# One decoder layer on one core: the values of key groups 0 and 1 as one Strassen product, and another order at the seam of the last two groups

## The chip, the cores and the metric

The kernel runs on one core of a Trainium2 chip. The metric is device time in microseconds for one launch, lower being better. The time before is 1264.26 us, the median of three runs (1264.23 to 1265.07).

## What is computed

One transformer layer on a sequence of 1024 tokens of width 512, all in float32: attention with 32 query heads and 8 key/value heads of 128 (four query heads share one key head, a group), rotary embedding and a causal mask; an addition and a layer norm; a gated feed-forward block of 1792; an addition and a second layer norm. Cut to what matters here:

```python
q = (x @ wq).reshape(B, T, H, HD).transpose(0, 2, 1, 3)
k = (x @ wk).reshape(B, T, KV, HD).transpose(0, 2, 1, 3)
v = (x @ wv).reshape(B, T, KV, HD).transpose(0, 2, 1, 3)
q = q * cos + _rotate_half(q) * sin
k = k * cos + _rotate_half(k) * sin
k = jnp.repeat(k, H // KV, axis=1)
v = jnp.repeat(v, H // KV, axis=1)
scores = jnp.einsum('bhtd,bhsd->bhts', q, k) * (1.0 / np.sqrt(HD))
scores = jnp.where(mask, scores, -jnp.inf)
att = jax.nn.softmax(scores, axis=-1)
out = jnp.einsum('bhts,bhsd->bhtd', att, v)
out = out.transpose(0, 2, 1, 3).reshape(B, T, H * HD) @ wo
x = _layernorm(x + out)
x = _layernorm(x + ffn(x))
```

## The kernel before

**Projections by Strassen's form.** The sequence is cut into two halves of 512 columns (blocks of 128 tokens, the odd ones in the first half, the even ones in the second) and the width of 512 into two halves. `blocks` holds a11, a12, a22 and four sums s1 to s4 of x; s3 lies over a21. `project_two(s)` (line 487) makes a pair of heads or groups from one product of two 2x2 block matrices: seven products in the order 1, 2, 6, 5, 3, 7, 4, each of two chunks of 128, with sums u1 to u4 of the weights. `weigh(s)` (line 262) makes u1, u2 and u3 on GpSimd; u4 follows after product 2. `steps` is the list of such pairs, `load(s)` fetches the weights of one. A product is added up by VectorE (`put`, lines 513 to 558), its first one copied by ScalarE (line 544). For values the operands are swapped, so that each product is 4 blocks of 128 columns.

**Plain projections.** The pairs in `PLAIN` (heads 0 to 3 of group 0, heads 2 and 3 of group 7), the keys of groups 0 and 7, and the values of groups 0 and 1 are made without it, half by half: `project_queries`, `project_keys` (with `rotate`, three VectorE instructions and a GpSimd add), and `values(g, even)` (line 375), each half of which is 4 blocks of 4 chunks of 128 columns, one ScalarE copy (line 391) and, after the first half, a GpSimd subtract of the weights (`difference`, line 284).

**Attention.** For each of 8 groups, the eight blocks of 128 queries are taken in the order 7, 1, 5, 3, 4, 2, 6, 0 (`ORDER`; p is the place in it, i the block). A block has four tiles t = 4i to 4i+3 of 32 tokens by 4 heads. `scores` (line 589) makes one tile: score matmuls into one of two PSUM buffers (`pair`), VectorE's masked minimum (line 609), ScalarE's exponential (626), VectorE's reciprocal (630), ScalarE's scaling (631) and a VectorE transpose by 32 x 32 blocks (634) into the buffer `turned`. When a block's four tiles are there, `gather` issues 16 DMAs on SyncE (line 684) that bring it from `turned` to `moved`, where two blocks lie at a time (`place`). After landing, matmuls with v make `o`, ScalarE copies it (856), and a pair of blocks is multiplied with wo (`project_pair`) and added to `sums`.

**Order.** TensorE's matmuls keep the program's order; the other engines' instructions are ordered by the framework's scheduler at build time, within the limits of dependencies and `issue_after`. A planner written out in the kernel chooses the program's order. It counts in units: one unit is one product of 128 x 128 by 512 columns. `Early` holds the projections that are still to be made for the next group, `Late` the blocks whose gather is under way. After each tile's scores, `run` (groups 0 to 5) or `deal` (groups 6 and 7) takes units from both. `weight` spreads the work over the 32 tiles of a group: the tile t gets 1 - share + 2 share (t + 1) / 33, with share 0.25 and, in the last two groups, 0.5. `make_room(g, p, i)` finishes all blocks whose place in `moved` the block i will take; it is called ahead of the block's last tile. Group 6 keeps three pairs of blocks (`held`) for group 7, which has no projections of a next group, to fill its time with.

**Start.** Before the attention loop come the first half of heads 0 to 3 and both halves of group 0's keys, then `values(0, 0)`. The other three halves of the values, and the second half of the heads, run between the first tiles. The three sums s3, s2 and s4 (line 1016) are made by VectorE as block p = 1 of group 0 begins.

Of the kernel before, what the change touches and what calls it, by code (L numbers as in the profile page):

```python
# [31 lines left out]
ALU = mybir.AluOpType  # L32
# [3 lines left out]
P = 128  # L36
# [4 lines left out]
KV = 8  # L41
HD = 128
REP = HEADS // KV
INNER = 1792
NT = T // P
# [26 lines left out]

HEAVY = 33 + 36 + NT // 2 * PAIR


# [19 lines left out]
def kernel(  # L95
# [88 lines left out]
    with ExitStack() as att:  # L184
# [66 lines left out]

        steps = []
        for g in range(KV - 2):
# [116 lines left out]

        current = added = None

        SOME = NT // 2 * NC * HD / W

        def values(g, even):

            nonlocal added
            if g not in vs:
                vs[g] = piece(f"v{g}").rearrange("p (j f) -> p j f", j=NT)
            pv = mbank(f"v_ps{g}_{even}")  # L380
            for j in range(NT // 2):
                for c, (w, x) in enumerate(operands(wvs[g], even)):
                    matmul(
                        pv[:, j * HD : (j + 1) * HD],
                        lhsT=x[:, j * P : (j + 1) * P],
                        rhs=w,
                        start=(c == 0),
                        stop=(c == NC - 1),
                    )
                if j == NT // 2 - 1:  # L390
                    nc.scalar.copy(
                        vs[g][:, 1 - even :: 2, :], pv.rearrange("p (j f) -> p j f", f=HD)
                    )
                    if not even:

                        with tc.issue_after(added.ins):
                            added = difference(wvs[g])
                yield NC * HD / W

# [4 lines left out]
        def rotate(dst, src, even, name):  # L404

            nonlocal added
            ts = slice(even * W, (even + 1) * W)
            b = ap.tile([P, W], F32, tag="rope_b", name=f"{name}_b{even}")


            def swapped():
                for to, of in ((slice(0, 64), slice(64, P)), (slice(64, P), slice(0, 64))):
                    nc.vector.tensor_tensor(
                        alike(b, dst)[to], src[of], alike(sin[:, ts], dst)[of], ALU.mult
                    )

            nc.vector.tensor_tensor(dst, src, alike(cos[:, ts], dst), ALU.mult)
            swapped()
            added = nc.gpsimd.tensor_tensor(dst, dst, alike(b, dst), ALU.add)
# [60 lines left out]
        def project_queries(g, head, even):  # L480
            dst = queries(g, even)[:, :, head, :]
            yield from project(dst, wqs[g * REP + head], even, f"q{g}_{head}", g > 0)
            if g == 0 and even and head % 2:
                load(head // 2 + 1)

        def project_two(s):
# [34 lines left out]
            for k, w, x in products:  # L521
# [21 lines left out]
                if k == 1:  # L543
                    nc.scalar.copy(v, ps[1])
                elif k == 2:
                    nc.gpsimd.tensor_tensor(u4, b21, u2, ALU.subtract)
                    put(c := out(0, 0), ps[2], alike(v, c))
                    done(0, 0)
                elif k == 6:
                    nc.vector.tensor_tensor(v, ps[6], v, ALU.add)  # L550
                elif k == 5:
                    put(c := out(1, 0), ps[5], alike(v, c))
                elif k == 3:
                    put(c := out(1, 0), ps[3], c)
                    done(1, 0)
                    weigh(s + 1)
                elif k == 7:
                    nc.vector.tensor_tensor(v, ps[7], v, ALU.add)
                    put(c := out(1, 1), ps[5], alike(v, c))
                    done(1, 1)  # L560
                else:
                    put(c := out(0, 1), ps[4], alike(v, c))
                    done(0, 1)
                    if s:
                        load(s + 2)
                yield 1

        def projections(g):


            s, pieces = 3 * (g - 1), []
            if g < KV - 1:
                pieces.append((PAIR * 2, project_two(s)))
            else:
                pieces += [(NC, project_keys(g, even)) for even in range(2)]
            for n in (2 * g, 2 * g + 1):
                s += 1
                if n in PLAIN:
                    pieces += [(NC, project_queries(g, 2 * (n % 2) + h, 0)) for h in range(2)]
                else:  # L580
                    pieces.append((PAIR * 2, project_two(s)))
            return pieces
# [316 lines left out]
        now = queue = 0.0  # L899
        late, tiles = deque(), []  # L900

# [35 lines left out]
        def run(g, until, early, pace, must=0, least=0, limit=None):  # L937
# [22 lines left out]
            while early.done < must:  # L960
                now += early.step()

        for piece_of in (
            project_queries(0, 0, 0),
# [4 lines left out]
            project_queries(0, 3, 0),  # L969
            values(0, 0),  # L970
        ):
            for _ in piece_of:
                pass

        with tc.issue_after(added.ins):
            for a in range(REP):
                added = difference(wqs[a])
        list(first_keys)
        weigh(0)
        for g in range(KV):  # L980
            todo, own, odd = [], 0, math.inf
            if g == 0:
                todo += [(SOME, values(*which)) for which in ((0, 1), (1, 0), (1, 1))]
            for a in range(REP):
                if (g * REP + a) // 2 in PLAIN:
                    todo.append((NC, project_queries(g, a, 1)))
# [11 lines left out]
            slots = T // Q  # L998
            slot = (early.total - own + HEAVY) / slots

            share = 0.25 if g < KV - 2 else 0.5
            weight = [1 - share + share * 2 * (t + 1) / (slots + 1) for t in range(slots)]
# [3 lines left out]
            for p, i in enumerate(ORDER):  # L1006

                for n in {0: (0,) if g % 2 else (0, 2), 4: (1,)}.get(p, ()):
                    while chores[n]:
                        current = current or chores[n]  # L1010
                        chore()
                if g == KV - 1 and p == 1:
                    load_wo(g)
                if g == 0 and p == 1:
                    for a in ((s3, a11, a21), (s2, s1, a11), (s4, a12, s2)):
                        chores[0].append(lambda a=a: nc.vector.tensor_tensor(*a, ALU.subtract))
                if g == 0 and 0 < p <= NT // 2:
# [6 lines left out]
                for b in range(B):  # L1024
                    t = i * B + b
                    if b == B - 1:
                        make_room(g, p, i)
# [3 lines left out]
                    now += (t + 1) * Q / W  # L1031
                    if b == B - 1:
                        tiles.append(Late(g, i, gather(g, p, i, x), now, unturned))
                        late.append(tiles[-1])
                    due += slot * weight[t]
                    passed += weight[t]
# [7 lines left out]
                    else:  # L1044
                        limit = early.total - (KEPT if g == KV - 1 else 0)
                        coming = [
                            ((k + 1) * B + LAG - done, Late.units(g, ORDER[k]))
                            for k in range(p + (b == B - 1), len(ORDER))
                        ]
# [423 lines left out]
```

## Time and profile before

| what | us |
|---|---|
| median of three runs | 1264.26 |
| the profiled execution | 1267.03 |
| its span, first to last instruction | 1265.2 |
| TensorE busy in it | 1247.5 |
| VectorE busy | 881.4 |
| ScalarE busy | 466.2 |
| GpSimd busy | 471.9 |
| mean granted TensorE clock | 0.997 |

The projections before the loop take the first 31 us, group 0 goes on to about 130 us, the seam of groups 6 and 7 lies near 875 us, the last scores near 975 us, the feed-forward block between 1005 and 1265 us. A line of the timeline gives start, length, engine, line, operation, names and count, and in brackets how long the engine had been idle and what ended it; matmuls are issued from one helper and all carry line 135. A list of waits gives total, number of times and the longest. A busy engine need not be at its peak: matmuls are pipelined and their ends are modelled.

### The profile page before, as it was taken

Reading aid. Unit: us, or ns where it says so; the run is one execution under the profiler, and the core shown is the slowest. Engines: PE = TensorE matmul, PEld = TensorE weight load, DVE = VectorE, ACT = ScalarE, POOL = GpSimd, SP = SyncE. Lnnn points to the kernel's source line nnn. Section 1 sums busy time; section 2 is a strip of 40 time slices with the busy share of each in tenths; the row PEclk is TensorE's granted clock in tenths of the full one; section 3 lists DMA queues with packets and bytes.
Section 4 is the critical chain, followed back from the end, with each engine's and each line's share of the span. In section 5 each row is a group of like instructions: output and inputs, shape, how many; then the busy total and the mean of one; then the engine's idle time right before and its main releaser. Section 6 shows DMA issues by size and latency. Waiting matters only on the chain. (4 is left out here: it accounts for less than half of the span.)

```text
span 1265.2 us, 14259 instructions
## 1 busy us (share of the span) xinstructions
PE 1247.5 (99%) x4142; PEld 735.9 (58%) x4142; DVE 881.4 (70%) x1821; ACT 466.2 (37%) x922; POOL 471.9 (37%) x708
## 2 busy tenths in 40 slices
PE   9999999999999999999999999999999999999998
PEld 5644676565456755655567555554656744444887
DVE  4677786887778767877796778687765674436743
ACT  0443344434443444444444444454555111111000
POOL 3541333343434233425341424253320756543321
PEclk9999999999999999999999999999999999999999
DMA  8243235433534344334433433544443711110000
GB/s 274 47 121 92 52 80 140 105 83 83 134 94 99 78 116 103 90 82 124 99 84 87 132 91 68 133 118 108 99 100 92 209 34 51 50 34 1 17 17 34
DMA packets 89326, 115.55 MB, mean 91 GB/s; under 512 B 18464, under 2 KB 60192, under 8 KB 89248
## 3 DMA queue, kind: packets, MB, share of 16 engines
q1 hardware_dynamic: 88240, 112.66, 35.4%
q10 hardware_dynamic: 1008, 1.97, 0.4%
q8 instruction: 34, 0.56, 0.2%
q14 instruction: 44, 0.36, 0.1%
HBM read 37.23 MB, written 2.10 MB: 31 GB/s over the span
## 5 line engine op out<-in xcount | busy, mean ns | idle before, releaser
L626 ACT ACTIVATE p<-s,low 128x928 f32<-128x928 f32 (+31 forms) x256 | 179.2, 700 | 362.1 <-DVE low L609 351.8
L634 DVE STREAM_TRANSPOSE turned<-p 128x1024 f32<-128x1024 f32 (+7 forms) x244 | 186.8, 775 | 101.5 <-ACT p L631 62.4
L135 PE MATMUL o<-moved,v 128*128 128x512 f32 x550 | 255.1, 597 | 0.0
L631 ACT ACTIVATE p<-p,share 128x928 f32<-128x928 f32 (+31 forms) x256 | 187.3, 735 | 120.8 <-DVE share L630 120.8
L609 DVE CUSTOM_DVE_ANT_0 s<-s,mask 128x928 f32<-128x928 f32 (+31 forms) x256 | 179.0, 700 | 56.5 <-PE s L135 54.8
L135 PE MATMUL s<-k,queries 128*128 128x512 f32 (+15 forms) x576 | 204.0, 464 | 2.3 <-ACT p L626 2.3
L135 PEld LDWEIGHTS s<-k,queries 128*128 128x128 f32 x576 | 108.5, 191 | 108.5 <-issue 96.3
L135 PEld LDWEIGHTS o<-moved,v 128*128 128x128 f32 x550 | 103.0, 191 | 104.5 <-issue 98.3
L135 PE MATMUL q_p<-blocks,wq 128*128 128x512 f32 x260 | 123.7, 594 | 0.0
L440 POOL TENSOR_TENSOR queries<-queries,q_b 128x512 f32<-128x512 f32 x52 | 71.3, 1371 | 122.1 <-DVE queries L439 115.6
L624 POOL MEMSET p<- 128x96 f32 (+2 forms) x192 | 26.3, 151 | 212.1 <-DVE turned L634 186.9
L135 PE MATMUL y<-wo,oT 128*128 128x256 f32 x428 | 103.7, 381 | 0.0
L135 PEld LDWEIGHTS y<-wo,oT 128*128 128x128 f32 x428 | 79.8, 190 | 21.5 <-issue 7.8
L434 DVE TENSOR_TENSOR q_b<-queries,sin 64x512 f32<-64x512 f32 x104 | 84.4, 811 | 3.1
L630 DVE RECIPROCAL share<-total 128x1 f32<-128x1 f32 x256 | 39.6, 155 | 57.7 <-ACT p L626 55.6
L135 PEld LDWEIGHTS q_p<-blocks,wq 128*128 128x128 f32 x260 | 48.4, 190 | 46.3 <-issue 40.5
L135 PE MATMUL s<-kT,queries 128*128 128x512 f32 (+8 forms) x192 | 68.3, 466 | 4.7 <-ACT p L626 4.7
L781 DVE TENSOR_TENSOR sums<-y,sums 128x512 f32<-128x512 f32 x112 | 66.9, 607 | 4.2 <-PE y L135 3.2
L135 PE MATMUL y<-u,os 128*128 128x256 f32 x224 | 57.5, 390 | 1.6 <-POOL os L760 1.6
L135 PEld LDWEIGHTS s<-kT,queries 128*128 128x128 f32 x192 | 35.7, 190 | 39.7 <-issue 29.2
L135 PE MATMUL q_p<-blocks,uq 128*128 128x512 f32 x104 | 49.8, 592 | 0.0
L626 ACT ACTIVATION_READ_ACCUMULATOR p<-s,low 128x1 f32 x256 | 49.5, 193 | 0.0
(273 smaller groups left out, 1771.2 us busy)
## 6 DMA issues: line engine op xcount, KB each, us to landing
moved<-turned SPq DMA_DIRECT2D x112, 128.0 KB, 2.4
moved<-turned SPq DMA_DIRECT2D x128, 112.0 KB, 2.2
moved<-turned SPq DMA_DIRECT2D x112, 96.0 KB, 2.2
moved<-turned SPq DMA_DIRECT2D x112, 80.0 KB, 2.1
wo<-wo SPq DMA_DIRECT2D x16, 512.0 KB, 4.5
moved<-turned SPq DMA_DIRECT2D x128, 64.0 KB, 2.0
wq<-wq SPq DMA_DIRECT2D x14, 512.0 KB, 4.4
moved<-turned SPq DMA_DIRECT2D x128, 48.0 KB, 1.9
```

Source lines behind the costliest of these rows:

```text
L135: tc.keep_in_program_order(nc.tensor.matmul(*args, **kw))
L434: nc.vector.tensor_tensor(alike(b[0], dst)[to], dst[of], alike(sin[:, ts], dst)[of], ALU.mult)
L440: nc.gpsimd.tensor_tensor(dst, dst, alike(b[0], dst), ALU.add)
L609: extreme = nc.vector.tensor_tensor_reduce(out=s[:, :n], in0=s[:, :n], in1=mask[:, T - n :], scale=1.0, scalar=MASKED, op0=ALU.add, op1=AL ...
L624: cleared = nc.gpsimd.memset(p[:, n:full], 0.0)
L626: nc.scalar.activation(p[:, :n], s[:, :n], AF.Exp, bias=low, scale=-1.0, accum_out=total)
L630: nc.vector.reciprocal(share, total)
L631: last_of_all = nc.scalar.activation(p[:, :n], p[:, :n], AF.Copy, scale=share)
L634: nc.vector.transpose(x[:, :, :, b, :].rearrange("p b j q -> p j b q"), p[:, :full].rearrange("p (j b k) -> p j b k", b=B, k=Q),)
L781: pin(nc.vector.tensor_tensor(to, out, to, ALU.add))
```

## The change

The values of groups 0 and 1 become the first entry of `steps`, so that every later index is one higher. `values` goes; `project_two(0)` takes its place: two of its seven products (four calls of `next`) ahead of the loop, the rest (10 units) between the first tiles. `weigh(0)` now makes the sums for the values, ahead of them, and `weigh(1)` those for the next pair. The sums s3 and s2 move to VectorE's place behind the rotations of the first half of the keys and of their second half, tied there by `issue_after`; s4 is handed to the first tile's chores. In the seam, `narrow` tells in groups 6 and 7 whether a block's place still holds more than one unit of unfinished work; if so, `make_room` and `gather` wait until the next block's first tile has its scores (`waiting`, which also carries over from group 6 to group 7). Of the two plain half-heads that group 7 made in its own time, the second half of head 2 moves into group 6; that of head 3 stays. The share in the last two groups goes from 0.5 to 0.1, and from group 1 on the work that `slot` spreads is 4 units larger (`AHEAD`).

```diff
@@ -71,6 +71,8 @@
+AHEAD = 4
@@ -249,7 +251,8 @@
-        steps = []
+        steps = [("v", 0, 1)]
         for g in range(KV - 2):
@@ -368,34 +371,7 @@
-        current = added = None
-        SOME = NT // 2 * NC * HD / W
-        def values(g, even):
-            nonlocal added
-            if g not in vs:
-                vs[g] = piece(f"v{g}").rearrange("p (j f) -> p j f", j=NT)
-            pv = mbank(f"v_ps{g}_{even}")
-            for j in range(NT // 2):
-                for c, (w, x) in enumerate(operands(wvs[g], even)):
-                    matmul(
-                        pv[:, j * HD : (j + 1) * HD],
-                        lhsT=x[:, j * P : (j + 1) * P],
-                        rhs=w,
-                        start=(c == 0),
-                        stop=(c == NC - 1),
-                    )
-                if j == NT // 2 - 1:
-                    nc.scalar.copy(
-                        vs[g][:, 1 - even :: 2, :], pv.rearrange("p (j f) -> p j f", f=HD)
-                    )
-                    if not even:
-                        with tc.issue_after(added.ins):
-                            added = difference(wvs[g])
-                yield NC * HD / W
+        current = added = moved = None
@@ -403,14 +379,15 @@
-            nonlocal added
+            nonlocal added, moved
             ts = slice(even * W, (even + 1) * W)
...
             def swapped():
+                nonlocal moved
                 for to, of in ((slice(0, 64), slice(64, P)), (slice(64, P), slice(0, 64))):
-                    nc.vector.tensor_tensor(
+                    moved = nc.vector.tensor_tensor(
                         alike(b, dst)[to], src[of], alike(sin[:, ts], dst)[of], ALU.mult
@@ -481,7 +458,7 @@
             if g == 0 and even and head % 2:
-                load(head // 2 + 1)
+                load(head // 2 + 2)
@@ -553,7 +530,8 @@
                     done(1, 0)
-                    weigh(s + 1)
+                    if s:
+                        weigh(s + 1)
                 elif k == 7:
@@ -561,14 +539,14 @@
                     done(0, 1)
-                    if s:
+                    if s > 1:
                         load(s + 2)
...
-            s, pieces = 3 * (g - 1), []
+            s, pieces = 3 * (g - 1) + 1, []
             if g < KV - 1:
@@ -576,7 +554,9 @@
                 if n in PLAIN:
-                    pieces += [(NC, project_queries(g, 2 * (n % 2) + h, 0)) for h in range(2)]
+                    which = (2, 0), (3, 0), (2, 1)
+                    pieces += [(NC, project_queries(g, *which_of)) for which_of in which]
                 else:
@@ -897,7 +877,15 @@
         now = queue = 0.0
-        late, tiles = deque(), []
+        late, tiles, waiting = deque(), [], None
+        def narrow(g, p, i):
+            if g < KV - 2 or g == KV - 1 and p == NT - 1:
+                return False
+            there = place(g, p, i)
+            return sum(l.left for l in tiles if not l.weighed and overlap(l.place, there)) > 1
@@ -960,6 +948,7 @@
+        sums_of_x = [1, (s3, a11, a21), (s2, s1, a11)]
         for piece_of in (
@@ -967,22 +956,35 @@
             project_queries(0, 3, 0),
-            values(0, 0),
         ):
...
+            if sums_of_x:
+                wait = sums_of_x[0]
+                if wait:
+                    sums_of_x[0] -= 1
+                else:
+                    with tc.issue_after(moved.ins):
+                        nc.vector.tensor_tensor(*sums_of_x[1], ALU.subtract)
+                    sums_of_x = [1] + sums_of_x[2:] if sums_of_x[2:] else []
+        weigh(0)
+        first_values = project_two(0)
+        for _ in range(4):
+            next(first_values)
...
         list(first_keys)
-        weigh(0)
+        weigh(1)
         for g in range(KV):
...
             if g == 0:
-                todo += [(SOME, values(*which)) for which in ((0, 1), (1, 0), (1, 1))]
+                todo.append((PAIR * 2 - 4, first_values))
             for a in range(REP):
-                if (g * REP + a) // 2 in PLAIN:
+                if (g * REP + a) // 2 in PLAIN and (g == 0 or a == REP - 1):
                     todo.append((NC, project_queries(g, a, 1)))
@@ -996,9 +998,9 @@
             slots = T // Q
-            slot = (early.total - own + HEAVY) / slots
-            share = 0.25 if g < KV - 2 else 0.5
+            slot = (early.total - own + HEAVY + (0 if g else AHEAD)) / slots
+            share = 0.25 if g < KV - 2 else 0.1
             weight = [1 - share + share * 2 * (t + 1) / (slots + 1) for t in range(slots)]
@@ -1009,11 +1011,10 @@
                         chore()
+                if g == 0 and p == 0:
+                    chores[0].append(lambda: nc.vector.tensor_tensor(s4, a12, s2, ALU.subtract))
                 if g == KV - 1 and p == 1:
                     load_wo(g)
-                if g == 0 and p == 1:
-                    for a in ((s3, a11, a21), (s2, s1, a11), (s4, a12, s2)):
-                        chores[0].append(lambda a=a: nc.vector.tensor_tensor(*a, ALU.subtract))
                 if g == 0 and 0 < p <= NT // 2:
@@ -1023,15 +1024,22 @@
                     t = i * B + b
-                    if b == B - 1:
+                    if b == B - 1 and not narrow(g, p, i):
                         make_room(g, p, i)
...
                     now += (t + 1) * Q / W
-                    if b == B - 1:
-                        tiles.append(Late(g, i, gather(g, p, i, x), now, unturned))
+                    if waiting or b == B - 1 and not narrow(g, p, i):
+                        g_of, p_of, i_of, x_of, at = waiting or (g, p, i, x, now)
+                        make_room(g_of, p_of, i_of)
+                        y, at = gather(g_of, p_of, i_of, x_of), max(at, now - TURNED)
+                        tiles.append(Late(g_of, i_of, y, at, unturned))
                         late.append(tiles[-1])
+                        waiting = None
+                    elif b == B - 1:
+                        waiting = g, p, i, x, now
                     due += slot * weight[t]
@@ -1045,7 +1053,7 @@
                             ((k + 1) * B + LAG - done, Late.units(g, ORDER[k]))
-                            for k in range(p + (b == B - 1), len(ORDER))
+                            for k in range(p + (b == B - 1 and not waiting), len(ORDER))
                         ]
```

## The prediction

> **What bounds the kernel now.** The page's first part says where to look: TensorE is busy nearly throughout.
>
> ```profile
> PE 1247.5 (99%) x4142; PEld 735.9 (58%) x4142; DVE 881.4 (70%) x1821; ACT 466.2 (37%) x922; POOL 471.9 (37%) x708
> ```
>
> So only two things can shorten it: fewer matmuls, or less time in which TensorE stands. The list of TensorE's waits gives the second.
>
> ```profile
> PE s L135 <- ACT p L626: 7.0, 4, 2.3
> PE y L135 <- POOL os L760: 1.6, 5, 0.4
> PE v_ps L135 <- POOL wv L284: 0.4, 1, 0.4
> ```
>
> Four waits of a score matmul for the exponential two tiles back (the `pair` tag has two PSUM buffers) make 7.0 us. TensorE's timeline places them, with the work that the change removes (start, length, engine, instructions; in brackets the idle time before).
>
> ```profile
> 32.50 2.84 PE L135 MATMUL v_ps<-wv,blocks 128*128 128x128 f32 x24
> 35.18 1.77 PE L135 MATMUL s<-kT,queries 128*128 128x512 f32 x4
> ...
> 43.94 1.60 PE L135 MATMUL v_ps<-wv,blocks 128*128 128x128 f32 x12 [0.41 <-POOL wv L284]
> ...
> 58.83 1.40 PE L135 MATMUL s<-kT,queries 128*128 128x512 f32 x4 [0.65 <-ACT p L626]
> ...
> 862.48 4.46 PE L135 MATMUL o<-moved,v 128*128 128x512 f32 x10
> 866.77 1.81 PE L135 MATMUL s<-k,queries 128*128 128x512 f32 x6
> 870.90 1.06 PE L135 MATMUL s<-k,queries 128*128 128x64 f32 x4 [2.32 <-ACT p L626]
> 871.75 4.12 PE L135 MATMUL o<-moved,v 128*128 128x512 f32 x6
> ...
> 901.44 0.82 PE L135 MATMUL s<-kT,queries 128*128 128x224 f32 x2 [1.87 <-ACT p L626]
> ...
> 968.18 1.02 PE L135 MATMUL o<-queries,v 128*128 128x512 f32 x2
> ...
> 971.51 0.73 PE L135 MATMUL s<-kT,queries 128*128 128x64 f32 x4 [2.17 <-ACT p L626]
> ```
>
> An instruction here is half a float32 product (two passes), so x24 is twelve calls; the planner's unit is two passes of 512 columns. Three of the four waits lie in the seam of groups 6 and 7. Cutting the span into stretches shows a second loss there (each row: stretch, length, busy time of PE, PEld, DVE, ACT and POOL, then the granted clock).
>
> ```profile
> 865.00:875.00 10.00, 7.68 (x20) 4.02 (x19) 7.47 (x20) 4.90 (x14) 1.72 (x4) 0.83 0.22 52
> 900.00:910.00 10.00, 8.56 (x29) 6.61 (x30) 6.22 (x21) 5.04 (x14) 3.15 (x8) 0.83 0.77 170
> 965.00:975.00 10.00, 7.83 (x25) 4.01 (x24) 5.12 (x17) 6.48 (x16) 0.00 (x0) 1.00 0.10 25
> ```
>
> After the stalls of 2.32 and 1.87 us the clock falls: 0.17 x 10 us = 1.7 us lost each time (the six `o` passes at 871.75 cover 4.12 us; the same count at 972.21 covers 2.81). After 2.17 us it does not. The seam thus holds 6.36 us of idle time and 3.4 us of half clock.
>
> **The change part by part.** The sum is made on the profiled execution, 1267.03 us (span 1265.2); the median shown is 2.77 lower, and I carry the difference over.
>
> *Values.* Before: 4 halves x 4 blocks x 4 chunks = 64 products, 128 passes. After: 7 products x 4 blocks x 2 chunks = 56, 112 passes. The 24 passes from 32.50 give way to a score at 35.18: 2.68/24 = 0.112 us. 16 x 0.112 = **-1.79 us**. Nothing else on TensorE is added or removed.
>
> *Waits that go with it.* `difference(wvs[1])` vanishes, and with it the 0.41 us at 43.94. The three subtracts of line 1016 took 1.77 + 1.22 + 2.09 = 5.08 us of VectorE between 50.5 and 60.2, just ahead of the stall of 0.65 us at 58.83; two now run before the scores and the third during tile 28. Between 0 and -0.65; I take all, because VectorE was between two of them when that stall built up. Together **-1.06**.
>
> *The price at the start.* `s3` and `s2` now stand on VectorE among the first rotations, behind k0's and k1's. Its idle gaps there are 1.17 us (before 23.92) and 1.34 (before 27.35), 2.51 together; the two subtracts need 2 x 1.22 = 2.44. That hides them with nothing to spare: queued behind them are the rotations of q1, k1, q2, q3, and for q3's the first score at 30.84 waits, which today starts 0.1 us after the `v_ps` passes end. If a GpSimd add gets in first, a subtract takes up to 2.09 (the longest of the three), 0.9 more each. On GpSimd, `weigh(0)` puts three subtracts (0.80 + 0.83 + 0.80, lines 277 to 279) where q3's add (29.53 to 30.79) is due; its gap before that add is 2.17 us, partly usable, so 0 to 1.5 us. `u4` (0.8) and one difference of 0.73 fewer hide in GpSimd's idle 63%; uncovered they would delay the wq differences, which TensorE needs only at 48.8. ScalarE loses four copies of 0.59 and gains one. VectorE gains seven adds of 0.69 (line 514's rows) and `s4`, 6.0 to 6.6 us, in the four widest tiles: their reductions (4 x 1.3), reciprocals and transposes (4 x 1.25) make 10.8, together some 17.2 us in the 17.3 from 32.7 to 50. Full, but a score is two buffers deep. Bounds 0 and +3.8 (0.9 x 2 + 1.5 + 0.5 for lag); I take **+0.8**, near the covered end, since every wait named has room today. The DMAs keep their order: `steps` grows by one and every index with it; weights of v0 and v1 were loaded before too.
>
> *Seam, stall at 870.90.* Today `make_room` runs ten `o` passes (4.29 us) before score 27, nothing stands between scores 27, 0 and 1, and score 1 waits for the exponential of 27. With `narrow` true there (five units of tile 4 unweighed), score 27 goes ahead and the ten passes land between scores 0 and 1. From the end of score 27 (868.4) to its release (870.9) is 2.5 us; 4.29 covers that. Lost: 2.32 idle and 1.7 of clock. What is late next is scores 2 and 3, now with thinner cover: 0.5. **-3.5**, bounds -4.0 and 0.
>
> *Stall at 901.44.* Score 6 waits for VectorE, which runs four transposes of 1024 columns in one go:
>
> ```profile
> 895.97 4.62 DVE L634 STREAM_TRANSPOSE turned<-p 128x1024 f32<-128x1024 f32 x4 [0.24 <-issue]
> ```
>
> Their buffer is free once tile 6's gather has been read: 16 DMAs at 0.63 us, 10.1 us on SyncE from 873.35. Score 27 is some 4 us earlier after the change, hence its last transpose and that gather too. But group 7's own projections shrink from 8 to 4 units (head 2 moves to group 6: 8 passes, 3.44 us, with its rotation of 2.1 us and its add of 1.3), so scores 28 to 31 also come sooner, and the four transposes may bunch again. Bounds -3.6 (1.87 + 1.7) and 0; I take half, **-1.8**.
>
> *Stall at 971.51.* `narrow` is not true there; only `share` 0.1 helps. The weight of tile 0 rises from 0.52 to 0.91 and that of tile 27 falls from 1.35 to 1.07, so that one unit (0.86 us) should fall between scores 0 and 1. Bounds -2.17 and 0; **-0.9**.
>
> *Deferred gathers and AHEAD.* A deferred gather is issued after one more score and its fill, some 3.3 us (99 us of group 7 over 32 tiles). On SyncE the next gather, and group 7's `wo` load, queue behind it; but the gather waits for the fourth transpose anyway (873.35 against score 27's end at 868.4), which hides most of it. AHEAD lifts the middle groups' rate from 139/32 to 143/32 units a tile; their rows are busy 119.5 us in 120, so little is there to win or lose. Bounds -0.5 and +6 (two gathers uncovered); **+1.0**.
>
> Sum: -1.79 - 1.06 + 0.8 - 3.5 - 1.8 - 0.9 + 1.0 = **-7.25**: 1259.8 for an execution like the profiled one, **1257.0** for the median.
>
> [...]
>
> **Rivals.** *The seam gives nothing* (its stalls only move): -1.79 - 1.06 + 0.8, that is 1262.2. For it: work there is conserved, and fill is what was lacking. Against it: ten passes demonstrably stand on the wrong side of score 27.
>
> *The seam gives all:* -2.05 - 4.0 - 3.6 - 2.2 = 1252.4. Against it: the third stall has no new cover but the flatter weights.
>
> *Slower, by the transposes at group 7's start.* If tile 6's gather does not begin earlier, scores 28 to 31 arrive 3.44 us sooner at transposes that stay where they are, the deferral adds 3.3, and the stall at 901.44 grows by 6.7 and drags a second slow window (1.7). With the first stall's gain kept: -2.05 - 3.5 + 8.4 = +2.9, 1267.1. It decides once the last transpose of tile 27 is less than about 3 us earlier relative to score 28. For it: today's four in a row. Against it: score 27 moves by 4.29.
>
> *That the change doesn't do what it says* would show as 128 passes still; the loop counts exclude it.
>
> **How the numbers follow.** Forecast 52% (own range 1253 to 1261), seam gives nothing 22%, gives all 11%, slower 15%. A difference under 0.2% (2.5 us) can't be told from none. Faster: 0.50 + 0.09 (a seam that gives a little) + 0.11 = 0.70; same 0.15; slower 0.15. The range 1251.5 to 1265 leaves out the slower case and a few per cent below.
>
> **What would show it.** 112 passes of `v_p` before group 1's, no wait on `wv`, no idle over 0.5 us before 60; ten `o` passes between scores of 32 and 64 columns near 860; no stretch at clock 0.83; four transposes no longer in a row near 892. First scores later than 31.5, or a wait over 2 us on `L626` in groups 6 and 7, would make it wrong.

## The result, and the profile after

| | before | after |
|---|---|---|
| median, us | 1265.54 (six runs, 1264.23 to 1266.67) | 1260.12 (six runs, 1259.84 to 1260.50) |
| profiled execution, us | 1267.03 | 1259.86 |
| its span, us | 1265.2 | 1257.8 |
| mean granted TensorE clock | 0.997 | 0.999 |

The ratio of the times is 0.9956, with a 95% interval of 0.9946 to 0.9966: the changed kernel is faster by 0.34 to 0.54%. The first part of its page (engine, busy us, share of the span, instructions):

```profile
PE 1242.7 (99%) x4126; PEld 733.3 (58%) x4126; DVE 889.5 (71%) x1828; ACT 464.1 (37%) x919; POOL 476.3 (38%) x710
```

There are 16 passes fewer on TensorE (4142 before), as counted. Its list of waits (total us, times, longest):

```profile
PE s L137 <- ACT p L606: 5.3, 7, 1.6
PE y L137 <- POOL os L740: 1.4, 4, 0.4
...
PE y L137 <- ACT oT L836: 0.7, 1, 0.7
```

The matmul helper is now line 137, the exponential line 606. The scores' four waits of 7.0 us have become seven of 5.3. TensorE's timeline places the larger ones (start, us, engine, instructions; in brackets the idle time before and what ended it).

```profile
27.44 3.73 PE L137 MATMUL v_p<-wv,blocks 128*128 128x128 f32 x32
31.16 1.82 PE L137 MATMUL s<-kT,queries 128*128 128x512 f32 x4
...
55.26 0.70 PE L137 MATMUL s<-kT,queries 128*128 128x256 f32 x2 [0.51 <-ACT p L606]
...
856.59 2.74 PE L137 MATMUL o<-moved,v 128*128 128x512 f32 x6
859.17 1.67 PE L137 MATMUL s<-k,queries 128*128 128x512 f32 x4
860.67 1.88 PE L137 MATMUL o<-moved,v 128*128 128x512 f32 x4
862.39 0.30 PE L137 MATMUL s<-k,queries 128*128 128x32 f32 x2
...
865.58 0.43 PE L137 MATMUL s<-k,queries 128*128 128x64 f32 x2 [1.09 <-ACT p L606]
...
870.72 0.49 PE L137 MATMUL s<-k,queries 128*128 128x128 f32 x2 [0.99 <-ACT p L606]
...
909.56 1.56 PE L137 MATMUL s<-kT,queries 128*128 128x512 f32 x4 [1.57 <-ACT p L606]
...
963.89 0.46 PE L137 MATMUL s<-kT,queries 128*128 128x96 f32 x2 [0.35 <-ACT p L606]
```

Of the ten `o` passes that stood ahead of score 27, six still do, and four now follow it. (Scores are counted by their tile in the group, 0 to 31; score 28 comes first and score 3 last.) The single stall of 2.32 us before score 1 has become 1.09 before score 1 and 0.99 before score 3; that of 1.87 is gone; in place of 2.17 before score 1 of group 7 there is 0.35 before score 2; and one of 1.57 us at 909.56 is new. The stretches that answer to those of before (stretch, length, busy PE, PEld, DVE, ACT, POOL, granted clock, DMA share, GB/s):

```profile
865.00:875.00 10.00, 8.43 (x24) 4.10 (x25) 7.57 (x25) 5.41 (x17) 3.94 (x8) 1.00 0.41 91
900.00:910.00 10.00, 8.43 (x36) 6.36 (x35) 4.99 (x13) 3.81 (x9) 8.53 (x16) 1.00 0.69 155
955.00:965.00 10.00, 9.65 (x33) 5.58 (x32) 5.89 (x16) 5.95 (x13) 0.00 (x0) 1.00 0.26 62
```

Both stretches at clock 0.83 are gone. In the second one GpSimd is busy for 8.53 of 10 us, against 3.15 before. That is where the new stall comes from, as the timeline of all engines shows:

```profile
905.09 0.73 POOL L742 TENSOR_TENSOR held<-held 128x256 f32<-128x256 f32 x1
...
905.77 0.73 POOL L743 TENSOR_TENSOR os<-held,os 128x256 f32<-128x256 f32 x1
...
906.44 0.33 POOL L604 MEMSET p<- 128x96 f32 x3
906.65 0.98 DVE L614 STREAM_TRANSPOSE spare<-p 128x768 f32<-128x768 f32 x1 [3.09 <-POOL p L604]
...
907.56 0.87 DVE L589 CUSTOM_DVE_ANT_0 s<-s,mask 128x704 f32<-128x704 f32 x1
...
908.57 0.85 ACT L606 ACTIVATE p<-s,low 128x704 f32<-128x704 f32 x1 [4.11 <-DVE low L589]
```

Read it upwards from the exponential. It waited 4.11 us for the minimum (L589), the minimum stood on VectorE behind a transpose, the transpose waited 3.09 us for the small zeroing of the unused columns of `p` (L604, 0.33 us for three), and the zeroing stood on GpSimd behind eleven adds, which run without a gap from 898.82 to 906.50: seven that conclude a pair of rows in `sums` (L703 to L709) and four that add up held blocks (L740 to L743).

**Where the time went.** For every pass the distance to the next pass's start is taken, less the usual distance at full clock for its width (0.112 us for 128 columns, 0.2155 for 256, 0.4293 for 512). The rest is loss: idle time, half clock, and small gaps. Group stretches begin at the group's first score, the last one at the first pass of the feed-forward block.

```
us                   start  group 0  groups 1-5  group 6  group 7  rest |  work   loss
before                3.31   2.19      9.74       4.71     7.38   0.17 | 1230.3  27.50
after                 3.63   1.38      7.85       3.14     5.69   0.17 | 1228.6  21.87
after, again (a2)     3.40   1.38      8.89       3.17     5.75   0.17 | 1228.6  22.76
e1_values             3.44   1.38      8.19       4.97     7.95   0.17 | 1228.6  26.11
e2_seam               3.43   2.19      8.69       3.15     6.06   0.17 | 1230.3  23.70
e3_nonarrow           3.55   1.28      8.46       3.72    10.50   0.17 | 1228.6  27.68
e4_share              3.59   1.39      8.80       7.21     7.92   0.17 | 1228.6  29.07
e5_head               3.50   1.28      7.97       9.08     9.05   0.17 | 1228.6  31.05
e6_ahead              3.54   1.64     14.08       5.31     6.20   0.17 | 1228.6  30.95
e7_memset             3.79   1.38      8.24       3.17     4.21   0.17 | 1228.6  20.96
e8_share_neg          3.32   1.39      8.28       1.42     4.71   0.17 | 1228.6  19.30
e9_both               3.34   1.49      7.50       1.65     4.23   0.17 | 1228.6  18.39
```

From before to after: work -1.7, start +0.3, group 0 -0.8, groups 6 and 7 -3.3, groups 1 to 5 -1.9. Of the last, about 1 us is spread between executions: `e2_seam` leaves groups 1 to 5 as in the kernel before and has 8.69 there, and the changed kernel's second profile has 8.89.

### The profile page after: what moved, and what is told of

The parts are those of the page before. It is cut to its first block, busy times and chain, and to the rows that moved or that the text cites. A ratio compares the mean times of both kernels' runs of the same rounds, so it can differ in the third digit from the quotient of the medians.

```text
span 1257.8 us, 14249 instructions
## 1 busy us (share of the span) xinstructions
PE 1242.7 (99%) x4126; PEld 733.3 (58%) x4126; DVE 889.5 (71%) x1828; ACT 464.1 (37%) x919; POOL 476.3 (38%) x710
## 5 line engine op out<-in xcount | busy, mean ns | idle before, releaser
L589 DVE CUSTOM_DVE_ANT_0 s<-s,mask 128x928 f32<-128x928 f32 (+31 forms) x256 | 179.0, 700 | 36.4 <-PE s L137 34.9
L604 POOL MEMSET p<- 128x96 f32 (+2 forms) x192 | 26.5, 150 | 222.1 <-DVE turned L614 198.0
```

What stands on the lines that cost most here:

```text
L589: extreme = nc.vector.tensor_tensor_reduce(out=s[:, :n], in0=s[:, :n], in1=mask[:, T - n :], scale=1.0, scalar=MASKED, op0=ALU.add, op1=AL ...
L604: cleared = nc.gpsimd.memset(p[:, n:full], 0.0)
```

## The experiments

All were timed in five rounds beside the kernel before, in three sets on three chips. The medians of before were 1266.82 us (33 runs, 1264.35 to 1269.15) for e1 to e4, 1267.14 (15 runs) for a2, e6, e7 and e8, and 1266.35 (15 runs) for e5, e9, e10 and e11. The changed kernel itself ran beside them in the second set alone (`a2_again`, ratio 0.9948). What e3, e4 and e5 cost against it is worked out from the ratio of the result, 0.9956; by 0.9948 each would cost 1.0 us more.

### The two halves of the change, alone

`e1_values` is the changed kernel with the seam as before: the values, the early sums and `AHEAD` stay.

```diff
-            if g < KV - 2 or g == KV - 1 and p == NT - 1:
-                return False
+            return False
...
-                    which = (2, 0), (3, 0), (2, 1)
+                    which = (2, 0), (3, 0)
...
-                if (g * REP + a) // 2 in PLAIN and (g == 0 or a == REP - 1):
+                if (g * REP + a) // 2 in PLAIN:
...
-            share = 0.25 if g < KV - 2 else 0.1
+            share = 0.25 if g < KV - 2 else 0.5
```

> The change without its seam: no deferral, share 0.5 and head 2 of group 7 as before; the Strassen values, the order at the start and AHEAD stay. My theory: all that the traces of before and after differ by until group 6 (4.15 us at the wait of group 5's first os, 769.21 against 765.06) stays, so 4 us below before, and the stalls of 2.3, 1.9 and 2.2 us in the seam are back. Rival, the values bring their 16 passes alone: 1.8 us below before. Rival, the seam is the whole gain: no difference from before.

Measured: 1263.95 us, ratio 0.9979 (0.9970 to 0.9988), 2.9 us under before: between the theory (4) and the first rival (1.8). Its stretches around the three old stalls:

```profile
865.00:875.00 10.00, 8.12 (x19) 3.94 (x20) 5.36 (x21) 5.36 (x16) 0.73 (x5) 0.83 0.35 79
890.00:900.00 10.00, 8.13 (x28) 4.70 (x27) 7.16 (x16) 4.71 (x10) 0.28 (x2) 1.00 0.20 44
963.00:973.00 10.00, 7.83 (x24) 4.32 (x23) 4.66 (x16) 5.54 (x17) 0.00 (x0) 0.83 0.27 61
```

The stalls are back, but the clock now falls after the first and the third, where in the kernel before it fell after the first and the second. The stalls are the same, and the clock answers to others of them: more on this at the end.

`e2_seam` is the kernel before with `narrow`, `waiting`, the moved half-head and share 0.1.

```diff
+        def narrow(g, p, i):
+            if g < KV - 2 or g == KV - 1 and p == NT - 1:
+                return False
...
-                    pieces += [(NC, project_queries(g, 2 * (n % 2) + h, 0)) for h in range(2)]
+                    which = (2, 0), (3, 0), (2, 1)
...
-            share = 0.25 if g < KV - 2 else 0.5
+            share = 0.25 if g < KV - 2 else 0.1
```

> The seam alone on the kernel before: deferral, share 0.1, head 2's second half in group 6; values by the plain product. My theory: 1.5 to 3.5 us below before, the rest of what the whole change gives. Rival, the seam needs the earlier part to line up: no difference or slower. If the two parts add up, this gain and that of the values alone make the 5.4 us of the whole.

Measured: 1263.65 us, 0.9979 (0.9971 to 0.9988), 3.2 us under before. The halves add up to 6.1 us, the whole change brought 5.4: they are close to independent, and each has about half of the gain.

### The parts of the seam, each undone

`e3_nonarrow` never defers a gather; all else is as after.

```diff
-            if g < KV - 2 or g == KV - 1 and p == NT - 1:
-                return False
+            return False
```

> The changed kernel without the deferral: narrow is always false, share 0.1 and the moved head stay. My forecast's theory, that the deferral takes the ten passes out of the way of score 27: 2 to 4 us slower than the changed kernel, with a stall of over 2 us at score 1 of group 6 again. Rival, the flatter share alone spreads the fill: within 0.7 us of the changed kernel.

Measured: 1265.12 us, 0.9989 (0.9981 to 0.9998); the changed kernel has 0.9956, so the deferral is worth 0.0033, some 4.2 us. TensorE's timeline in the seam:

```profile
859.60 4.45 PE L137 MATMUL o<-moved,v 128*128 128x512 f32 x10
863.89 1.67 PE L137 MATMUL s<-k,queries 128*128 128x512 f32 x4
...
868.58 0.43 PE L137 MATMUL s<-k,queries 128*128 128x64 f32 x2 [1.09 <-ACT p L606]
...
874.64 1.82 PE L137 MATMUL s<-kT,queries 128*128 128x512 f32 x4 [1.68 <-ACT p L606]
...
897.67 0.84 PE L137 MATMUL s<-kT,queries 128*128 128x224 f32 x2 [1.87 <-ACT p L606]
...
966.88 0.43 PE L137 MATMUL s<-kT,queries 128*128 128x64 f32 x2 [2.17 <-ACT p L606]
```

The ten passes stand ahead of score 27 again, and yet the wait at score 1 is 1.09 us, the same as with the deferral. So the deferral is not what halved the old stall of 2.32. Nor can it be put down to one of the other parts: score 1 of group 6 waits 0.81 us with the old share (`e4_share`) and 0.88 with the half-head back in group 7 (`e5_head`), and 2.32 only where all three parts are undone (`e1_values`). With the share, the deferral or the half-head undone alone, one or two products of `q_ps` stand between scores 0 and 1; in `e1_values` nothing does. The deferral pays later: without it score 28 of group 7 waits 1.68 and the two old stalls of group 7 return (1.87 and 2.17), which the table shows as 10.50 against 5.69.

`e4_share` puts the share back.

```diff
-            share = 0.25 if g < KV - 2 else 0.1
+            share = 0.25 if g < KV - 2 else 0.5
```

> The changed kernel with share 0.5 in the last two groups instead of 0.1; deferral and moved head stay. If the flat share is what spreads the fill over the small tiles: 2 to 4 us slower, with stalls over 1.5 us at scores 1 of groups 6 and 7. If the deferral does it: within 0.7 us, and the stall in group 7 alone is back (1 us).

Measured: 1266.70 us, 1.0005 (0.9996 to 1.0013): the whole gain of the change is gone, 0.0049 or 6.2 us. That is more than the 2 to 4 us expected. Its seam in TensorE's timeline:

```profile
872.73 0.49 PE L137 MATMUL s<-k,queries 128*128 128x128 f32 x2 [0.85 <-ACT p L606]
876.02 3.43 PE L137 MATMUL s<-kT,queries 128*128 128x512 f32 x4 [2.81 <-ACT p L606]
```

The long stall is not at score 1, where it was expected (0.81 us there), but at group 7's first score: scores 3 and 28 follow each other with nothing between them. After 2.81 us of waiting the four passes of score 28 take 3.43 us, twice the 1.72 that they take in the changed kernel: the clock is at half.

`e5_head` gives group 7 the second half of head 2 back.

```diff
-                    which = (2, 0), (3, 0), (2, 1)
+                    which = (2, 0), (3, 0)
...
-                if (g * REP + a) // 2 in PLAIN and (g == 0 or a == REP - 1):
+                if (g * REP + a) // 2 in PLAIN:
```

> The changed kernel with the second half of head 2 of group 7 back in group 7's own time; deferral and share 0.1 stay. If the moved head feeds the end of group 6 and relieves the start of group 7: 1 to 3 us slower than the changed kernel (ratio to before 0.9965 to 0.998), with longer waits near scores 1 and 3 of group 6. If it only moves 3.44 us of matmuls: within 0.5 us of it (0.995 to 0.9956).

Measured: 1267.19 us, 1.0009 (1.0000 to 1.0018), some 6.7 us above the changed kernel by the ratios, where 1 to 3 were expected. All engines' timeline shows why:

```profile
868.99 1.88 PE L137 MATMUL q_ps<-blocks,wq 128*128 128x512 f32 x4
...
872.58 0.65 DVE L394 TENSOR_TENSOR queries<-q_ps,cos 128x512 f32<-128x512 f32 x1
...
873.24 1.39 DVE L390 TENSOR_TENSOR q_b<-q_ps,sin 64x512 f32<-64x512 f32 x2
...
874.71 1.25 POOL L396 TENSOR_TENSOR queries<-queries,q_b 128x512 f32<-128x512 f32 x1 [1.88 <-DVE q_b L390]
...
876.02 3.46 PE L137 MATMUL s<-kT,queries 128*128 128x512 f32 x4 [5.14 <-POOL queries L396]
```

The last plain half-head that group 6 makes is one that group 7's first score needs, and VectorE begins its rotation only at 872.58, 1.7 us after the product's end (870.87); the add on GpSimd ends at 875.96. TensorE stands for 5.14 us. In the changed kernel the half that was moved is made last; it is needed only from group 7's block p = 4 on, so it stands between the needed half and the score.

`e6_ahead` sets the other constant back.

```diff
-AHEAD = 4
+AHEAD = 0
```

> The changed kernel with AHEAD 0, so that the middle groups spread 139 units over 32 tiles and not 143. If AHEAD only holds the order that was there: 0.5 to 2 us slower, with other waits of y for os in groups 1 to 5. If it does nothing for the time: within 0.5 us of the changed kernel.

Measured: 1269.51 us, 1.0019 (1.0010 to 1.0028), 8.7 us above the changed kernel beside it (`a2_again`, 1260.77), where 0.5 to 2 were expected.

The expectation has the constant in the wrong place, and so have the prediction and the section on the change. The code adds `(0 if g else AHEAD)`, so it counts in group 0 and is nothing from group 1 on. Group 0 spreads 167 units in the kernel before, 169 with `AHEAD` 4 and 165 with 0, since the new values leave it 10 units where the plain ones had 12; the middle groups spread 139 either way. The order of work parts from the changed kernel's halfway through group 0 (block p = 3), and the damage comes after it. TensorE's timeline at the seam of groups 1 and 2:

```profile
279.23 1.03 PE L137 MATMUL y<-wo,os 128*128 128x256 f32 x4
280.10 0.65 PE L137 MATMUL s<-k,queries 128*128 128x96 f32 x4
284.29 2.54 PE L137 MATMUL s<-k,queries 128*128 128x512 f32 x4 [3.54 <-POOL oT L742]
```

Two small scores and the next group's first follow each other without fill, and TensorE stands 3.54 us. (The profile names a GpSimd add as what ended the wait; the exponential of score 2, which frees the buffer, ended at about 284.05.) The changed kernel has sixteen `y` passes between the last two and twelve between the scores before them. That stall, the half clock behind it (1.7 us: the score takes 2.54 us and the eight `y` passes that follow it 2.88, against 1.72 and 1.89 for such work in the changed kernel) and a wait of 1.33 us at 225.73 cover what groups 1 to 5 lose more (14.08 against 8.89); group 6 loses 2.1 us more. Work to fill with was there: this kernel makes as many passes in group 0, but 24 fewer in groups 1 to 5 (2044 against 2068), all of them `y` passes of group 1, and makes them only in group 6. The planner held them back; how four units in group 0 lead to that is not shown.

### The new stall, and a further step

`a2_again` is the changed kernel once more, beside the others.

> The changed kernel once more, as the measure for the others of this row: 4.5 to 6 us below before. If the kernel before owes its spread (1264.35 to 1269.15) to half-clock windows after its stalls, these runs spread by less than 1.5 us and their mean clock stays at 0.999 to 1.0, since no stall in them is over 1.6 us.

Measured: 1260.77 us (1260.24 to 1260.86), 0.9948 (0.9935 to 0.9962). The five runs spread by 0.6 us, at a mean clock of 0.999 to 1.000, as the theory has it.

`e7_memset` takes the zeroing of `p` in group 7 away from GpSimd's queue.

```diff
-            cleared = nc.gpsimd.memset(p[:, n:full], 0.0)
+            cleared = (nc.vector if g == KV - 1 else nc.gpsimd).memset(p[:, n:full], 0.0)
```

> The changed kernel with the zeroing of p's masked end in group 7 on VectorE instead of GpSimd; nothing else. Theory, the new stall of 1.57 us at 909.56 comes from the transpose that waits for a zeroing queued behind the sums that conclude a pair of rows on GpSimd: that stall goes and the kernel is 0.8 to 1.6 us faster than the changed one. Rival, VectorE is late there by itself: the stall stays over 1 us and the time is the same.

Measured: 1258.63 us, 0.9931 (0.9919 to 0.9944), 2.1 us under `a2_again`, a little more than expected. TensorE's timeline:

```profile
908.38 1.45 PE L137 MATMUL s<-kT,queries 128*128 128x512 f32 x4
...
922.35 1.27 PE L137 MATMUL s<-kT,queries 128*128 128x512 f32 x4 [0.81 <-ACT p L606]
```

The score that waited 1.57 us now starts with no wait, and waits of 0.47 us at 918 and 0.31 at 942 are gone too; one of 0.81 us at 922 is new. The table has 1.5 us less loss in group 7 (5.75 to 4.21) for the 2.1 us of time. That the stall goes when only the zeroing moves shows its cause.

`e8_share_neg` flattens the weights further, past even, so that a small tile gets more fill than a large one.

```diff
-            share = 0.25 if g < KV - 2 else 0.1
+            share = 0.25 if g < KV - 2 else -0.1
```

> The changed kernel with share -0.1, so that small tiles get more fill than large ones. If more fill between small tiles is all that the seam needs: 0.5 to 1.5 us faster, with the stalls at scores 1 and 3 of group 6 (1.1 and 1.0 us) shorter. If the fill is now missed at the large tiles: as fast or slower, with new waits of score matmuls of more than 512 columns.

Measured: 1257.71 us, 0.9923 (0.9910 to 0.9935), 3.1 us under `a2_again`, where at most 1.5 were expected. TensorE's timeline:

```profile
861.84 2.82 PE L137 MATMUL q_ps<-blocks,wq 128*128 128x512 f32 x6
864.50 0.33 PE L137 MATMUL s<-k,queries 128*128 128x64 f32 x2
...
891.09 0.59 PE L137 MATMUL s<-kT,queries 128*128 128x192 f32 x2 [1.77 <-ACT p L606]
```

Six passes now stand ahead of score 1 where four did, and it no longer waits (score 0 waits 0.63); a wait of 1.77 us comes in group 7, behind VectorE's transposes, and the one at 909 is gone although the zeroing still is on GpSimd.

`e9_both` joins both edits.

```diff
-            cleared = nc.gpsimd.memset(p[:, n:full], 0.0)
+            cleared = (nc.vector if g == KV - 1 else nc.gpsimd).memset(p[:, n:full], 0.0)
...
-            share = 0.25 if g < KV - 2 else 0.1
+            share = 0.25 if g < KV - 2 else -0.1
```

> The changed kernel with share -0.1 and the zeroing of group 7 on VectorE, the two that gained alone (3.1 and 2.1 us). If they remove different stalls: 4 to 5 us below the changed kernel (ratio to before 0.990 to 0.991). If share -0.1 already avoids the queue on GpSimd (its trace has no wait near 908): the same as share -0.1 alone, 0.992.

`e10_both6` is e9 with the zeroing of group 6 moved too.

```diff
-            cleared = (nc.vector if g == KV - 1 else nc.gpsimd).memset(p[:, n:full], 0.0)
+            cleared = (nc.vector if g >= KV - 2 else nc.gpsimd).memset(p[:, n:full], 0.0)
```

> The same with the zeroing on VectorE in group 6 too. GpSimd is 37% busy and group 6 has none of the pair sums that made the queue: within 0.7 us of the one before. If GpSimd's rotations hold up the zeroing there as well: 0.7 to 2 us faster.

`e11_both_more` is e9 with share -0.3.

```diff
-            share = 0.25 if g < KV - 2 else -0.1
+            share = 0.25 if g < KV - 2 else -0.3
```

> As with both, but share -0.3. If more fill at the small tiles goes on paying: 0.5 to 1.5 us faster than with -0.1. If -0.1 is near the best: 0.5 to 3 us slower, with waits at large tiles.

Measured: e9 1256.24 us (1255.68 to 1256.68), 0.9921 (0.9908 to 0.9935); e10 1256.06, 0.9920 (0.9906 to 0.9933); e11 1260.23, 0.9950 (0.9938 to 0.9963). e9 and e10 are faster than both kernels of this study: the intervals of their ratios lie below the changed kernel's (0.9946 to 0.9966). By the ratio they aren't told from e8 (0.9923), which is the second of the two outcomes expected for e9: share -0.1 had removed the wait at 909 already, and moving the zeroing had little left to take. That group 6's zeroing makes no difference is as expected. One wait over 1 us stays in e9:

```profile
890.63 0.59 PE L137 MATMUL s<-kT,queries 128*128 128x192 f32 x2 [1.74 <-ACT p L606]
```

Share -0.3 overdoes it: e11 is 4.0 us slower than e9. Group 7 waits for GpSimd's sums of the blocks that it meant to fill with (TensorE's timeline of e11); that it has used up other work too early is likely, but not shown:

```profile
903.96 1.13 PE L137 MATMUL y<-u,os 128*128 128x256 f32 x4 [2.42 <-POOL os L741]
```

## Why the prediction was right, and where it was not

**Values (-1.79): right.** 112 passes of `v_p`, 0.112 us apart; the least time of all TensorE's work fell by 1.7 us.

**Waits that go with it (-1.06): three quarters.** The 0.41 us for `wv` is gone. The 0.65 us at 58.83 was put down to the three subtracts of line 1016. With these elsewhere, the score just ahead of that one waits 0.51 us (at 55.26): the minimum that it needs stands on VectorE behind two transposes (1.56 us) and a rotation (1.39). So nearly as much is lost without the subtracts, and how much of the 0.65 was theirs is not shown. Group 0's loss fell by 0.8.

**The price at the start (+0.8): about 0.** From the first pass of q to the first score took 25.71 us before (5.13 to 30.84) and 25.64 after (5.52 to 31.16). VectorE's gaps and GpSimd's idle time did hide the sums. The covered end of the bounds was the answer.

**The seam (-3.5 - 1.8 - 0.9 + 1.0 = -5.2): -3.3, and by another mechanism.** This is the step that failed. "The ten passes land between scores 0 and 1" did not happen: six stay ahead of score 27, four follow it, and the wait at score 1 is the same 1.09 us with the deferral and without. The idle time there fell only from 2.32 to 2.08 us; the gain is the half clock, which came after the wait of 2.32 and after neither of the two that replace it. The stall at 901.44 went wholly where half was taken, and that at 971.51 gave 1.8 where 0.9 was taken. There, "only `share` 0.1 helps" was wrong: with share 0.1 and no deferral the 2.17 us are back (`e3_nonarrow`). Against that stand new waits in group 7 that the prediction had not: 1.57, 0.47 and 0.31 us of scores, and 0.68 us of `y` for `oT`. For the first two it lacked the zeroing behind the adds on GpSimd: it priced what was queued on VectorE and SyncE behind the moved gathers, and GpSimd's queue it took, for the start, as idle at 63% over the whole span.

**Deferred gathers and AHEAD (+1.0), "so little is there to win or lose": mis-sized by far, part by part.** The rate of 143/32 for the middle groups is a misreading of the code: `AHEAD` counts in group 0 alone. Undone singly, `AHEAD` costs 8.7 us, the moved half-head 6.7, the share 6.2, the deferral 4.2. These sum to 25.8, nearly five times the whole gain: with one part undone, gaps open that neither the kernel before nor the changed one has (2.81 and 5.14 us at group 7's first score, 3.54 at group 2's), so the parts pay only together. The prediction saw the moved half only as work taken from group 7, with a rival in which that did harm; it is a cushion between a rotation and the score that needs it.

**The slower rival** (scores 28 to 31 too early at the transposes) did not come: three transposes still run in one go (886.72, 3.50 us on VectorE), but no score waits behind them over 1 us until the share goes to -0.1 (1.77 us in e8).

**The sum and the median.** The sum gave 1259.8 us for an execution like the profiled one, and the profiled one took 1259.86. That it came so close is luck: the seam brought 1.9 us less than forecast, while the start cost 0.8 less than forecast and groups 1 to 5 lost 0.9 to 1.9 us less than before, part of it spread. The step from there to the median was wrong: "the median shown is 2.77 lower, and I carry the difference over". Those 2.77 us are the kernel before's own spread, which goes with the mean clock that a run was granted (of 33 of its runs, one at 1264.35 was granted a mean clock of 1.000, those near 1265 0.998, those near 1267 0.997, and the one of 1269.15 0.995). The changed kernel has no half clock after its stalls (1.00 from 5.5 to 1254.6 us of its profile) and no such spread (1259.84 to 1260.50), so nothing was to be carried: 1257.0 forecast, 1260.12 measured. A gain of 3.4 us in clock was counted against a median of three runs that, by their times, had hardly paid all of it (their clocks are not on record).

**The signs.** Of those named, the ten `o` passes between scores of 32 and 64 columns did not come, and a wait of 0.51 us before 60 stands just over the bound of 0.5. The rest came as named: 112 passes of `v_p`, no wait on `wv`, no stretch at clock 0.83, three transposes in a row and not four.

**Left open:** how four units in group 0 (`AHEAD`) come to leave the end of group 1 without fill, when the kernel before did without them at 167 units (before with `AHEAD` was not tried, nor other values of it); what the three parts of the seam each do at score 1 of group 6; how much of the 0.9 to 1.9 us in groups 1 to 5 is real; the 1.74 us that are left in e9.

## What to carry to other kernels

Where a planner fills the gaps of one engine, look at what stands between neighbouring short pieces at each seam, and undo the constants one at a time: a part that looks like zero can carry the whole gain. Before calling an engine idle, look at its queue in the very stretch that the change fills: a memset of 0.15 us behind a row of adds cost 1.57 us. Read a constant's condition in the code before pricing it: `AHEAD` counted in another group than its author thought. And take the run-to-run spread of the kernel before apart before carrying a difference from one execution to the median.

## What the runs showed of the hardware

In the profiled execution of the kernel before, the clock was at half in two stretches between the first passes and the last: from 871.06 to 874.47 us and from 901.78 to 905.19. Each is 3.41 us long and costs half of that, 1.7 us, of work. Their starts lie 30.72 us apart, nine times that length. The first came after the stall of 2.32 us that ended at 870.90, the second after the one of 1.87 us that ended at 901.44; behind the stall of 2.17 us that ended at 971.51 the clock stayed at 1.00.

The other runs, with stalls behind which a view shows the clock or the pace:

| run | stall of TensorE, us | behind it |
|---|---|---|
| after | 1.57 | clock 1.00 (906 to 912 us) |
| e1_values | the three of before: 2.32, 1.87, 2.17 | clock 0.83 over 10 us (865 to 875), 1.00 (890 to 906), 0.83 (963 to 973) |
| e3_nonarrow | 1.68 | four score passes of 512 columns in 1.82 us, full clock |
| e4_share | 2.81 | such passes in 3.43 us, half clock |
| e5_head | 5.14 | such passes in 3.46 us, half clock |
| e6_ahead | 3.54 | such passes in 2.54 us, then eight `y` passes in 2.88: half clock for a part |
| e8_share_neg | 1.77 | two `o` passes in 1.02 us, full clock |
| e9_both | 1.74 | two `o` passes in 1.02 us, full clock |
| e11_both_more | 2.42 | four `y` passes in 1.13 us, full clock |

So the length of a stall alone doesn't decide: half clock came after 1.87 us in the kernel before and not after the same stall in `e1_values`, after 2.17 in `e1_values` and not in the kernel before, nor after 2.42 in e11. What decides is not shown.

Kernels with stalls of about 1.9 to 2.3 us spread more from run to run, most of the runs at lower mean clocks (before 1264.35 to 1269.15 us, mean clock 0.995 to 1.000; e1_values 1261.81 to 1266.03, 0.996 to 0.998; e3_nonarrow 1263.93 to 1266.41, 0.996 to 0.998), than one whose longest wait for an exponential is 1.6 (e2_seam 1263.20 to 1264.48, 0.999 to 1.000; eleven runs like e1 and e3).
